# Moving elementwise work to the scalar engine and sums over partitions back to the matrix engine in a four-layer graph network

## The chip, the cores and the metric

The kernel runs on one core of a Trainium2 chip. A core has five engines that each work through their own instruction stream in the order in which it was written: PE (TensorE, matmuls), DVE (VectorE, elementwise work and reductions), ACT (ScalarE, activations and copies), POOL (GpSimd, slower elementwise work[...]) and SP (here it only issues DMAs). They meet through semaphores. Matmul results land in PSUM, of which this kernel has eight buffers of 128 x 512 float32; everything else lives in SBUF.

The metric is the device time of one execution in microseconds, given as the median over runs. All arithmetic is float32.

## The reference, cut to what matters

64 independent graphs of 256 nodes with 256 features go through four layers, each of the form `x = layernorm(x + layer(x, adj))`. What the change touches, in the reference's own terms with the rest cut:

```python
# layer 0: leaky ReLU (slope 0.01) on three projections, sigmoid attention, normalized by degree
X = heads(lrelu(x @ W_lin + b_lin)); q = heads(lrelu(x @ W_q)); k = heads(lrelu(x @ W_k))
adj_h = adj[:, None] * sigmoid(q @ k.T * scale)          # 4 heads
deg = sum(adj_h, axis=-1); dis = where(deg > 0, deg ** -0.5, 0)
Y = (dis[..., :, None] * adj_h * dis[..., None, :]) @ X  # then a layernorm with gain and bias
# layer 1: masked softmax attention with 8 heads
scores = where(adj > 0, q @ k.T / sqrt(32), NEG)
# ...
# layer 2: neighbour sum, then an MLP of width 1024 with an RMS norm
h = agg @ W1 + b1
h = silu(h * rsqrt(mean(h * h, axis=-1) + 1e-6) * rms_weight); out = h @ W2 + b2
# layer 3: additive attention
e = s1[:, :, None] + s2[:, None, :]; e = where(e > 0, e, 0.2 * e); e = where(adj > 0, e, NEG)
h_prime = softmax(e) @ Wh
hn = (h_prime - mean) / sqrt(var + 1e-5) * gamma + beta; out = gelu(hn)
```

## The kernel before: the parts that matter

The kernel describes each graph's work as a list of operations, each with an engine, a cost that its author assigned, and the values it reads and writes. A list scheduler in the kernel then takes the operations of all 64 graphs together, picks at each step the one that can start first, and emits them in that order. So the order on each engine is fixed when the program is built, and several graphs at different layers are in flight at once. `"p"` values are PSUM buffers (eight), `"s"` values are SBUF buffers, `"h"` values are scratch in device memory.

```python
SLOTS = {"s": 42, "d": 10, "b": 3, "c": 72, "p": 8, "h": 8}

def transposed(src):                    # four 128x128 transposes on PE, into PSUM
    ps = Value("p", "ps", 2)
    transpose(lambda: two(ps), lambda: two(src), ps, src)
    return ps

def far_transposed(src, name):          # a transpose by DVE in 32x32 blocks, a DMA out and four DMAs back
    eb, far, dst = Value("s", "eb"), Value("h", "far"), Value("s", name, 4)
    op("DVE", 600, lambda: dve.transpose(...), [eb], [src])
    op("SP", 420, lambda: nc.sync.dma_start(far.t[:, :512], eb.t), [far], [eb], after=3000)
    for q in range(4):
        op("SP", 420, lambda q=q: nc.sync.dma_start(dst.t[...], far.t[...]), [(dst, q)], [far], after=4200)
    return dst

def normed(src, name):                  # layernorm: statistics on DVE, power -0.5 on POOL, apply on DVE
    mv, m = stats(src)
    dst = Value("s", name, 2)
    for n in range(NB):
        op("DVE", 328, lambda n=n: dve.tensor_scalar(two(dst)[:, n, :], two(src)[:, n, :],
           m()[:, n, 0:1], m()[:, n, 2:3], op0=OP.subtract, op1=OP.mult), [(dst, n)], [(src, n), mv])
    return dst

# ---- layer 0
for w, name in ((lambda: c.w0_q, "qT0"), (lambda: c.w0_k, "kT0")):
    ps = feature_major(w, xT)
    y = Value("s", name)
    op("ACT", 478, lambda ps=ps, y=y: act.activation(y.t, ps.t, AF.Copy, scale=0.01), [y], [ps])
    op("DVE", 608, lambda ps=ps, y=y: dve.tensor_tensor(y.t, ps.t, y.t, OP.max), [y], [ps, y])
# ... v likewise: bias on DVE, then max(0.01 v, v) on DVE
added = [Value("s", "added") for _ in range(H0 // 2)]
for i in range(2):                      # POOL adds the two halves of the key index
    op("POOL", 1220, lambda i=i, A2=A2: pool.tensor_tensor(two(added[i]), A2(0), A2(1), OP.add), ...)
def fn(ps=ps):                          # PE sums over partitions with a matrix of ones
    for h in range(H0):
        pe.matmul(ps.t[h * 32:(h + 1) * 32, :N], c.ones, two(added[h // 2])[:, h % 2], start=True, stop=True)
op("PE", PE_MM, fn, [ps], added, mode="columns")
# ...
yb = far_transposed(ps, "yT")
# ... two DVE multiplications by dis, each 128x256, then layernorm

# ---- between layers 0 and 1
op("DVE", 343, lambda: dve.tensor_scalar(adj.t, adj.t, 0.0, NEG, op0=OP.is_le, op1=OP.mult), [adj], [adj])

# ---- layer 2
for j in range(0, HB, 2):               # HB = 8
    # ... two blocks of W1 into ps, then
    op("DVE", 608, lambda ps=ps, j=j: dve.tensor_tensor(
        Hb(j, 2), two(ps), c.b2_1[:, j:j + 2, None].to_broadcast([P, 2, N]), OP.add), both, [ps])
    sq = Value("s", "sq")
    op("ACT", 532, lambda sq=sq, j=j: act.activation(two(sq), Hb(j, 2), AF.Square), [sq], both)
    sqs.append(sq)
    if len(sqs) % 2 == 0:               # POOL adds the squares of this pair and the one before
        op("POOL", 1220, lambda a=sqs[-2], sq=sq: pool.tensor_tensor(sq.t, sq.t, a.t, OP.add), [sq], [sq, sqs[-2]])
# then four matmuls with ones, one column group each

# ---- layer 3
# low3 = 0.2 * s1 on DVE; e = 0.2 * s2 + low3 on ACT; e = max(s2 + s1, e) on DVE
for n in range(NB):                     # 1/sum of the softmax
    op("DVE", 392, lambda n=n, ps=ps: dve.tensor_scalar(two(y3)[:, n, :], two(ps)[:, n, :], r3.t[:, n:n + 1], None,
                                                        op0=OP.mult), [(y3, n)], [(ps, n), r3])
mv, m = stats(y3)
affine(y3, mv, m, lambda: c.g3, lambda n: c.b3)
```

Of the kernel before, what the change touches and what calls it, by code (L numbers as in the profile page):

```python
# [10 lines left out]
AF = mybir.ActivationFunctionType  # L11
OP = mybir.AluOpType
# [151 lines left out]
def graph(plan, nc, c, t, out, b):  # L164
# [32 lines left out]
    def far_transposed(src, name):  # L197


        eb, far, dst = Value("s", "eb"), Value("h", "far"), Value("s", name, 4)  # L200
        op("DVE", 600, lambda: dve.transpose(
            eb.t.rearrange("p (b g i) -> p g b i", b=4, i=32),
            src.t.rearrange("p (n k w) -> p k n w", n=2, k=2)), [eb], [src])
        op("SP", 420, lambda: nc.sync.dma_start(far.t[:, :512], eb.t), [far], [eb], after=3000)
        for q in range(4):
            op("SP", 420, lambda q=q: nc.sync.dma_start(
                dst.t[32 * q:32 * q + 32].rearrange("j (a g) -> j a g", a=4),
                far.t[:, :512].rearrange("(a j) (b g) -> b j a g", a=4, b=4)[q]), [(dst, q)], [far], after=4200)
        return dst

    def spread(v):

        return v.t.rearrange("p (a j i w) -> p j i a w", a=4, j=2, i=2)

# [5 lines left out]
    def feature_major(w, xT, cols=None):  # L220

        ps = Value("p", "ps", 2)
        for o in range(2):
            def fn(o=o):
                for k in range(DB):
                    pe.matmul(two(ps)[:, o, :], w()[:, k, o * P:(o + 1) * P], (cols or two)(xT)[:, k],  # L226
                              start=(k == 0), stop=(k == DB - 1))
            op("PE", 2 * PE_MM, fn, [(ps, o)], [xT])
        return ps

    def token_major(xT, w, r=(), cols=None):

        ps = Value("p", "ps", 2)
        for n in range(NB):
            def fn(n=n):
                for k in range(DB):
                    pe.matmul(two(ps)[:, n, :], cols(xT)[:, k, n] if cols else two(xT)[:, k, n * P:(n + 1) * P], w()[:, k, :],  # L237
                              start=(k == 0), stop=(k == DB - 1))
            op("PE", 2 * PE_MM, fn, [(ps, n)], [xT, *r])
        return ps  # L240
# [4 lines left out]
    def stats(src):  # L245

        mv, st = Value("c", "mv", 2), Value("c", "st", 2)
        m = lambda: mv.t[:, :6].rearrange("p (n k) -> p n k", n=2)
        for n in range(NB):
            op("DVE", 311, lambda n=n: dve.bn_stats(st.t[:, 6 * n:6 * n + 6], two(src)[:, n, :]), [(st, n)], [(src, n)])  # L250
        for n in range(NB):
            op("DVE", 82, lambda n=n: dve.bn_aggr(m()[:, n, 0:2], st.t[:, 6 * n:6 * n + 6]), [(mv, n)], [(st, n)])  # L252

        def fn():
            pool.tensor_scalar(m()[:, :, 2], m()[:, :, 1], 1e-5, None, op0=OP.add)  # L255
            pool.tensor_tensor(m()[:, :, 2], m()[:, :, 2], c.mhalf[:, :NB], OP.pow)  # L256
        op("POOL", 1750, fn, [mv], [mv])
        return mv, m
# [20 lines left out]
    def affine(y, mv, m, g, add, r=()):  # L279

        for n in range(NB):
            op("DVE", 395, lambda n=n: dve.scalar_tensor_tensor(
                two(y)[:, n, :], two(y)[:, n, :], m()[:, n, 0:1], g(), op0=OP.subtract, op1=OP.mult),
                [(y, n)], [(y, n), mv])
# [21 lines left out]
    for w, name in ((lambda: c.w0_q, "qT0"), (lambda: c.w0_k, "kT0")):  # L306
        ps = feature_major(w, xT)
        y = Value("s", name)
        op("ACT", 478, lambda ps=ps, y=y: act.activation(y.t, ps.t, AF.Copy, scale=0.01), [y], [ps])
        op("DVE", 608, lambda ps=ps, y=y: dve.tensor_tensor(y.t, ps.t, y.t, OP.max), [y], [ps, y])  # L310
# [5 lines left out]
    op("DVE", 608, lambda: dve.scalar_tensor_tensor(v.t, v.t, 0.01, v.t, op0=OP.mult, op1=OP.max), [v], [v])  # L316
# [20 lines left out]
    added = [Value("s", "added") for _ in range(H0 // 2)]  # L337
    for i in range(2):
        A2 = lambda n, i=i: att.t.rearrange("p (h n c) -> p h n c", h=H0, n=NB)[:, 2 * i:2 * i + 2, n]
        op("POOL", 1220, lambda i=i, A2=A2: pool.tensor_tensor(two(added[i]), A2(0), A2(1), OP.add),  # L340
           [added[i]], [(att, 2 * i), (att, 2 * i + 1)])

    def fn(ps=ps):
        for h in range(H0):
            pe.matmul(ps.t[h * 32:(h + 1) * 32, :N], c.ones, two(added[h // 2])[:, h % 2], start=True, stop=True)
    op("PE", PE_MM, fn, [ps], added, mode="columns")
# [26 lines left out]
    yb = far_transposed(ps, "yT")  # L373
    y = Value("s", "y", 2)
    for i in range(2):
        by = lambda ap, i=i: ap.rearrange("p g (i k w) -> p g i k w", i=2, k=2)[:, :, i]
        op("DVE", 345, lambda y=y, i=i, by=by: dve.tensor_tensor(
            by(y.t.rearrange("p (g d) -> p g d", g=4)), yb.t.rearrange("p (i k g w) -> p i g k w", i=2, k=2, g=4)[:, i],
            dis.t[:, :8].rearrange("p (g i) -> p i g", i=2)[:, i, :, None, None].to_broadcast([P, 4, 2, 32]), OP.mult),
            [y], [yb, dis])  # L380
# [5 lines left out]
    op("DVE", 343, lambda: dve.tensor_scalar(adj.t, adj.t, 0.0, NEG, op0=OP.is_le, op1=OP.mult), [adj], [adj])  # L386
# [81 lines left out]
    for j in range(0, HB, 2):  # L468
        ps = Value("p", "ps", 2)
        for i in range(2):  # L470
# [6 lines left out]
        op("DVE", 608, lambda ps=ps, j=j: dve.tensor_tensor(  # L477
            Hb(j, 2), two(ps), c.b2_1[:, j:j + 2, None].to_broadcast([P, 2, N]), OP.add), both, [ps])
# [4 lines left out]
        if len(sqs) % 2 == 0:  # L483
            op("POOL", 1220, lambda a=sqs[-2], sq=sq: pool.tensor_tensor(sq.t, sq.t, a.t, OP.add), [sq], [sq, sqs[-2]])  # L484

    def fn(sqs=sqs):
        for i in range(4):
            pe.matmul(sums.t[i * 32:(i + 1) * 32, :N], c.ones, two(sqs[i // 2 * 2 + 1])[:, i % 2, :],
                      start=True, stop=True)
    op("PE", PE_MM, fn, [sums], [sqs[1], sqs[3]], mode="columns")  # L490
# [51 lines left out]
    low3 = Value("c", "low3")  # L542
    op("DVE", 50, lambda: dve.tensor_scalar(low3.t[:, :NB], V3()[:, :, D], 0.2, None, op0=OP.mult), [low3], [v3])
# [6 lines left out]

    e = Value("s", "e3", 2)
    for n in range(NB):
        op("ACT", 360, lambda n=n: act.activation(two(e)[:, n, :], ps2.t[:, :N], AF.Identity,
                                                  bias=low3.t[:, n:n + 1], scale=0.2), [(e, n)], [ps2, low3])
        op("DVE", 395, lambda n=n: dve.scalar_tensor_tensor(
            two(e)[:, n, :], ps2.t[:, :N], s1(n), two(e)[:, n, :], op0=OP.add, op1=OP.max),
            [(e, n)], [(e, n), ps2, v3])
# [6 lines left out]
    for n in range(NB):  # L564
        op("DVE", 392, lambda n=n, ps=ps: dve.tensor_scalar(two(y3)[:, n, :], two(ps)[:, n, :], r3.t[:, n:n + 1], None,
                                                            op0=OP.mult), [(y3, n)], [(ps, n), r3])
    mv, m = stats(y3)
    affine(y3, mv, m, lambda: c.g3, lambda n: c.b3)
# [140 lines left out]
```

## Time and profile before

| | |
|---|---|
| time, median of 3 runs | 3073.91 us (3069.96 to 3080.2) |
| span of the profiled run | 3068.2 us, mean granted clock of PE 0.980 |
| busy: PE, DVE, ACT, POOL | 2887.1, 2714.1, 1783.9, 1241.2 us |
| DMA | 412.31 MB, mean 134 GB/s |

A row of the group view reads: line of the kernel, engine, operation, output <- inputs, shape, count | busy time and mean nanoseconds of one | idle time of the engine just before these instructions, and what ended it. One float32 matmul in the source stands as two MATMUL instructions in the trace, each with its weight load (row PEld). Matmuls are pipelined: the trace gives each a length of about 380 ns, but they start 216 ns apart in a dense stretch, so the distance of the starts counts and not the length. PSUM buffers carry the name `ps` nearly everywhere.

### The profile page before, as it was taken

To read this page: it belongs to the slowest core of one execution; us is meant where nothing else is said; L and a number is where in the kernel's file an instruction comes from. 1 tells how busy PE (TensorE), PEld (TensorE's weight loads), DVE (VectorE), ACT (ScalarE), POOL (GpSimd) and SP (SyncE) were. 2 spreads that over 40 slices of the span, in tenths; PEclk is the share of its full clock that TensorE was granted. 3 is DMA by queue.
4 is the path that set the end of the run, shared out by engine and by line. 5 is a ranking of instruction groups with operands and counts; after the bars stand their busy time and mean duration, and the time that the engine had idled before them with its cause. 6 is when DMAs were issued, how large, how long until landed. Compare 5 with 4: busy or idle time off the path is not lost.

```text
span 3068.2 us, 55984 instructions
## 1 busy us (share of the span) xinstructions
PE 2887.1 (94%) x17860; PEld 2230.5 (73%) x17860; DVE 2714.1 (88%) x7693; ACT 1783.9 (58%) x4226; POOL 1241.2 (40%) x1478
## 2 busy tenths in 40 slices
PE   4899999999999999999999999998999999998986
PEld 3677777777778777777777777776777777776764
DVE  3879999999989989989788999988998999899874
ACT  1545656666556566655556656655566556555553
POOL 3234444444434434344334443443444443443322
PEclk8999999999999999999999999999999999999997
DMA  5444455443554445535353454354454455353440
GB/s 165 134 137 147 131 146 162 131 135 109 148 151 149 151 130 146 148 111 155 94 162 104 152 155 145 113 143 124 135 155 138 124 168 152 100 147 118 124 124 11
DMA packets 351766, 412.31 MB, mean 134 GB/s; under 512 B 42992, under 2 KB 310128, under 8 KB 351472
## 3 DMA queue, kind: packets, MB, share of 16 engines
q1 hardware_dynamic: 344064, 403.34, 44.8%
q10 hardware_dynamic: 7408, 5.39, 0.6%
q8 instruction: 144, 2.36, 0.3%
q14 instruction: 150, 1.23, 0.1%
HBM read 240.27 MB, written 168.30 MB: 133 GB/s over the span
## 4 chain that ended last, share of the span: by engine, by line
PE 56%; DVE 28%; DMA 7%; issue 2%; SPq 2%; ACT 2%; POOL 2%; DVEq 0%; POOLq 0%; ACTq 0%
PE ps L473 10%; PE ps L522 9%; PE ps L226 9%; PE ps L237 8%; PE ps L405 3%; PE ps L537 3%; DVE eb L417 3%; DVE st L250 3%; DVE x L264 2%; DVE e L294 2%; PE ps L370 2%; DVE att L334 2%; PE ps L327 2%; PE av L430 2%; DVE hT L509 2%
## 5 line engine op out<-in xcount | busy, mean ns | idle before, releaser
L299 ACT ACTIVATE e<-e,low 128x256 f32<-128x256 f32 x1152 | 573.7, 501 | 83.4 <-DVE low L294 82.2
L522 PE MATMUL ps<-L_gnn_W,hT 128*128 128x256 f32 x2048 | 481.7, 387 | 18.7 <-ACT hT L513 18.7
L473 PE MATMUL ps<-aggT,L_gnn_W 128*128 128x256 f32 x2048 | 480.1, 382 | 2.6 <-DVE hT L477 1.1
L522 PEld LDWEIGHTS ps<-L_gnn_W,hT 128*128 128x128 f32 x2048 | 383.9, 191 | 100.5 <-ACT hT L513 23.4
L473 PEld LDWEIGHTS ps<-aggT,L_gnn_W 128*128 128x128 f32 x2048 | 378.8, 190 | 67.9 <-issue 10.0
L294 DVE CUSTOM_DVE_ANT_0 e<-ps,adj 128x256 f32<-128x256 f32 x1024 | 363.7, 417 | 23.4 <-PE ps L405 22.8
L484 POOL TENSOR_TENSOR sq<-sq 128x512 f32<-128x512 f32 x128 | 168.5, 1317 | 483.6 <-ACT sq L480 477.2
L255 POOL TENSOR_SCALAR mv<-mv 128x2 f32<-128x2 f32 x384 | 123.7, 322 | 580.9 <-DVE mv L252 526.1
L417 DVE STREAM_TRANSPOSE eb<-e 128x1024 f32<-128x1024 f32 x256 | 310.5, 1222 | 8.2 <-ACT e L299 8.2
L256 POOL TENSOR_TENSOR mv<-mv,mhalf 128x2 f32<-128x2 f32 x384 | 297.4, 774 | 32.0
L250 DVE BATCH_NORM_STATS2 st<-y 128x6 f32<-128x256 f32 x768 | 288.6, 410 | 1.7
L271 POOL TENSOR_TENSOR xb<-x,b 128x512 f32<-128x512 f32 x128 | 175.5, 1372 | 213.2 <-DMA x<-in_x 140.3
L340 POOL TENSOR_TENSOR added<-att 128x512 f32<-128x512 f32 x128 | 179.5, 1406 | 158.8 <-DVE att L334 122.2
L299 ACT ACTIVATION_READ_ACCUMULATOR e<-e,low 128x1 f32 x1152 | 219.1, 190 | 0.0
L509 DVE SCALAR_TENSOR_TENSOR hT<-hT,r,pr 128x256 f32<-128x256 f32 x512 | 205.3, 473 | 7.4 <-PE pr L506 7.3
L334 DVE TENSOR_TENSOR att<-att,adjT 128x512 f32<-128x512 f32 x256 | 197.4, 798 | 13.1 <-DMA adjT<-in_adjT 7.7
L264 DVE TENSOR_SCALAR x<-y,mv 128x256 f32<-128x256 f32 x384 | 183.8, 506 | 16.5 <-POOL mv L256 16.5
L480 ACT ACTIVATE sq<-hT 128x512 f32<-128x512 f32 x256 | 157.8, 622 | 69.2 <-DVE hT L477 66.6
L217 ACT COPY xT<-ps 128x512 f32<-128x512 f32 x128 | 74.6, 582 | 196.2 <-PE ps L189 189.7
L477 DVE TENSOR_TENSOR hT<-ps,b 128x512 f32<-128x512 f32 x256 | 169.3, 681 | 14.5 <-PE ps L473 13.8
L332 ACT ACTIVATE att<-ps 128x512 f32<-128x512 f32 x256 | 135.6, 598 | 75.5 <-PE ps L327 75.0
L358 POOL TENSOR_TENSOR dp<-dp,mhalf 128x8 f32<-128x8 f32 x64 | 109.2, 1707 | 144.8 <-DVE dp L357 139.6
(109 smaller groups left out, 6136.3 us busy)
## 6 DMA issues: line engine op xcount, KB each, us to landing
far<-eb SPq DMA_DIRECT2D x256, 512.0 KB, 3.0
eT<-far SPq DMA_DIRECT2D x1024, 128.0 KB, 3.8
x0T<-in_xT SPq DMA_DIRECT2D x64, 256.0 KB, 4.1
adjT<-in_adjT SPq DMA_DIRECT2D x64, 256.0 KB, 4.1
x<-in_x SPq DMA_DIRECT2D x64, 256.0 KB, 4.4
adj<-in_adj SPq DMA_DIRECT2D x64, 256.0 KB, 3.9
far<-eb SPq DMA_DIRECT2D x64, 256.0 KB, 2.2
yT<-far SPq DMA_DIRECT2D x256, 64.0 KB, 2.2
```

Of the source, the lines that this page charges most:

```text
L226: pe.matmul(two(ps)[:, o, :], w()[:, k, o * P:(o + 1) * P], (cols or two)(xT)[:, k], start=(k == 0), stop=(k == DB - 1))
L237: pe.matmul(two(ps)[:, n, :], cols(xT)[:, k, n] if cols else two(xT)[:, k, n * P:(n + 1) * P], w()[:, k, :], start=(k == 0), stop=(k == DB ...
L250: op("DVE", 311, lambda n=n: dve.bn_stats(st.t[:, 6 * n:6 * n + 6], two(src)[:, n, :]), [(st, n)], [(src, n)])
L256: pool.tensor_tensor(m()[:, :, 2], m()[:, :, 2], c.mhalf[:, :NB], OP.pow)
L264: op("DVE", 328, lambda n=n: dve.tensor_scalar(two(dst)[:, n, :], two(src)[:, n, :], m()[:, n, 0:1], m()[:, n, 2:3], op0=OP.subtract, op1= ...
L294: op("DVE", 345, lambda n=n: dve.tensor_tensor_reduce(out=E(n), in0=two(logits)[:, n, :], in1=two(negmask)[:, n, :], scale=-scale, scalar= ...
L299: op("ACT", 491, lambda n=n: act.activation(E(n), E(n), AF.Exp, bias=low.t[:, n:n + 1], scale=-1.0, accum_out=r.t[:, col(n):col(n) + 1]), ...
L334: op("DVE", 608, lambda h=h: dve.tensor_tensor(A(h), A(h), two(adjT), OP.mult), [(att, h)], [(att, h), adjT])
L417: op("DVE", 1130, lambda e=e, eb=eb: dve.transpose(eb.t.rearrange("p (b g i) -> p g b i", b=4, i=32), e.t.rearrange("p (g b i) -> p g b i" ...
L473: pe.matmul(two(ps)[:, i, :], c.w2_1[:, k, (j + i) * P:(j + i + 1) * P], two(aggT)[:, k, :], start=(k == 0), stop=(k == DB - 1))
L509: op("DVE", 391, lambda j=j: dve.scalar_tensor_tensor(Hb(j)[:, 0], Hb(j)[:, 0], c.r2[:, j:j + 1], pr.t[:, :N], op0=OP.mult, op1=OP.mult), ...
L522: pe.matmul(two(ps)[:, n, :], Hb(j)[:, 0, n * P:(n + 1) * P], c.w2_2[:, j, :], start=(j == 0), stop=(j == HB - 1))
```

## The change

The change takes work off DVE and puts it on ACT, POOL and PE. (1) The leaky ReLUs of layer 0 and of layer 3 become one parametric-ReLU activation on ACT each. (2) The softmax's 1/sum in layer 3 is no longer multiplied into the rows; it enters the statistics of the norm that follows. (3) Layer 2's bias is added on ACT. (4) Layer 1's mask is made on POOL. In return three things that had relieved PE are gone: (5) the two additions on POOL ahead of layer 0's degree sums, (6) the two ahead of layer 2's sums of squares, and (7) layer 0's transpose by way of DVE and device memory, in whose place PE transposes.

```diff
-        op("ACT", 478, lambda ps=ps, y=y: act.activation(y.t, ps.t, AF.Copy, scale=0.01), [y], [ps])
-        op("DVE", 608, lambda ps=ps, y=y: dve.tensor_tensor(y.t, ps.t, y.t, OP.max), [y], [ps, y])
+        op("ACT", 478, lambda ps=ps, y=y: act.activation(y.t, ps.t, AF.Prelu, alpha=0.01), [y], [ps])
...
-    op("DVE", 608, lambda: dve.scalar_tensor_tensor(v.t, v.t, 0.01, v.t, op0=OP.mult, op1=OP.max), [v], [v])
+    op("ACT", 478, lambda: act.activation(v.t, v.t, AF.Prelu, alpha=0.01), [v], [v])
...
-        op("POOL", 1220, lambda i=i, A2=A2: pool.tensor_tensor(two(added[i]), A2(0), A2(1), OP.add),
-           [added[i]], [(att, 2 * i), (att, 2 * i + 1)])
...
-        for h in range(H0):
-            pe.matmul(ps.t[h * 32:(h + 1) * 32, :N], c.ones, two(added[h // 2])[:, h % 2], start=True, stop=True)
-    op("PE", PE_MM, fn, [ps], added, mode="columns")
+        for m in range(NB):
+            for h in range(H0):
+                pe.matmul(ps.t[h * 32:(h + 1) * 32, :N], c.ones, A(h)[:, m, :], start=(m == 0), stop=(m == NB - 1))
+    op("PE", 2 * PE_MM, fn, [ps], [att], mode="columns")
...
-    yb = far_transposed(ps, "yT")
+    ps = transposed(copy(ps, "yT"))
     y = Value("s", "y", 2)
-    for i in range(2):   # ... two multiplications by dis, from yb
+    op("DVE", 608, lambda ps=ps, y=y: dve.tensor_tensor(by_head(y.t), by_head(ps.t), dis_b(), OP.mult), [y], [ps, dis])
...
-    op("DVE", 343, lambda: dve.tensor_scalar(adj.t, adj.t, 0.0, NEG, op0=OP.is_le, op1=OP.mult), [adj], [adj])
+    op("POOL", 1100, lambda: pool.tensor_scalar(adj.t, adj.t, 0.0, NEG, op0=OP.is_le, op1=OP.mult), [adj], [adj])
...
-        op("DVE", 608, lambda ps=ps, j=j: dve.tensor_tensor(
-            Hb(j, 2), two(ps), c.b2_1[:, j:j + 2, None].to_broadcast([P, 2, N]), OP.add), both, [ps])
+        for i in range(2):
+            op("ACT", 357, lambda ps=ps, i=i, j=j: act.activation(
+                Hb(j + i)[:, 0], two(ps)[:, i, :], AF.Identity, bias=c.b2_1[:, j + i:j + i + 1]), [(hT, j + i)], [(ps, i)])
...
-        if len(sqs) % 2 == 0:
-            op("POOL", 1220, lambda a=sqs[-2], sq=sq: pool.tensor_tensor(sq.t, sq.t, a.t, OP.add), [sq], [sq, sqs[-2]])
...
+        if len(sqs) == 2:               # twice per graph: four matmuls with ones, summed up in one PSUM buffer
+            def fn(sqs=sqs, j=j):
+                for i in range(4):
+                    pe.matmul(sums.t[i * 32:(i + 1) * 32, :N], c.ones, two(sqs[i // 2])[:, i % 2, :],
+                              start=(j == 2), stop=(j == HB - 2))
...
-    op("DVE", 50, lambda: dve.tensor_scalar(low3.t[:, :NB], V3()[:, :, D], 0.2, None, op0=OP.mult), [low3], [v3])
...
-        op("ACT", 360, lambda n=n: act.activation(two(e)[:, n, :], ps2.t[:, :N], AF.Identity,
-                                                  bias=low3.t[:, n:n + 1], scale=0.2), [(e, n)], [ps2, low3])
-        op("DVE", 395, lambda n=n: dve.scalar_tensor_tensor(
-            two(e)[:, n, :], ps2.t[:, :N], s1(n), two(e)[:, n, :], op0=OP.add, op1=OP.max),
-            [(e, n)], [(e, n), ps2, v3])
+        op("ACT", 360, lambda n=n: act.activation(two(e)[:, n, :], ps2.t[:, :N], AF.Prelu, bias=s1(n), alpha=0.2),
+           [(e, n)], [ps2, v3])
...
-        op("DVE", 392, ...)             # y3 = ps * r3, twice
-    mv, m = stats(y3)
-    affine(y3, mv, m, lambda: c.g3, lambda n: c.b3)
+    mv, m = stats(ps, r3)               # three small DVE products put r3 into variance and scale
+    affine(y3, mv, m, lambda: c.g3, lambda n: c.b3, src=ps)
```

## The prediction

> **What bounds the kernel now.** I read the busy line of the page first, then the same engines cut into head, middle and tail, then the waits of PE, then the rows of each line that the change touches, and last a piece of PE's timeline.
>
> ```profile
> PE 2887.1 (94%) x17860; PEld 2230.5 (73%) x17860; DVE 2714.1 (88%) x7693; ACT 1783.9 (58%) x4226; POOL 1241.2 (40%) x1478
> ...
> core 0: us, PE busy (x) PEld busy (x) DVE busy (x) ACT busy (x) POOL busy (x), PEclk, DMA share, GB/s
> 0.00:200.00 200.00, 148.72 (x885) 110.01 (x886) 128.51 (x332) 75.38 (x179) 62.67 (x75) 0.91 0.50 145
> 200.00:2800.00 2600.00, 2522.71 (x15770) 1956.37 (x15769) 2392.11 (x6792) 1577.42 (x3752) 1099.18 (x1300) 0.99 0.47 139
> 2800.00:3068.00 268.00, 215.64 (x1208) 164.13 (x1207) 193.47 (x571) 131.07 (x296) 79.35 (x105) 0.90 0.28 85
> ```
>
> In the middle 2600 us PE is busy for 2522.7, that is 97%, and idle for only 77 us. DVE is at 92% there. Of PE's 181 idle us (3068.2 - 2887.1), 51 lie in the first 200 us (weights still arriving) and 52 in the last 268 (the last graphs have no others to hide behind). So the kernel is bound by PE, with DVE close behind as the engine that PE sometimes waits for:
>
> ```profile
> PE ps L189 <- DVE x L264: 34.9, 34, 3.7
> PE ps L327 <- DVE kT L310: 19.5, 1, 19.5
> PE ps L522 <- ACT hT L513: 18.7, 7, 5.7
> PE ps L657 <- DMA b_v<-in_L_gnn_bv: 18.2, 1, 18.2
> PE ps L189 <- DVE mv L252: 8.3, 4, 5.6
> ```
>
> Columns: who waits for whom, total us, how often, longest. The two single waits of 18 to 20 us belong to the start. What repeats is PE waiting for a normalized `x` (L264) before it can transpose it. The whole list is short: PE has enough other graphs to work on.
>
> ```profile
> 1004.65 6.21 PE L473 MATMUL ps<-aggT,L_gnn_W 128*128 128x256 f32 x28
> 1010.70 0.60 PE L189 MATMUL ps<-ident,e 128*128 128x128 f32 x4
> 1011.14 1.89 PE L226 MATMUL ps<-x0T,L_gnn_W_k 128*128 128x256 f32 x8
> ...
> 1015.55 0.64 PE L488 MATMUL sums<-sq,ones 128*32 128x256 f32 x8
> 1016.01 0.61 PE L345 MATMUL ps<-added,ones 128*32 128x256 f32 x8
> 1016.55 1.13 PE L237 MATMUL ps<-L_gnn_Wo,yT 128*128 128x256 f32 x4
> ```
>
> These are prices: start to next start, not the printed lengths. A full matmul instruction takes 6.05 / 28 = 216 ns, four transposes 0.44 us, eight instructions of a sum over partitions (four column groups at once, two passes) 0.46 us, or 0.54 when the array goes back to full matmuls afterwards.
>
> **What the Trainium skill says.** "Perfetto Trace Analysis", section Tensor Engine Instruction, says that the profiler estimates a matmul's end; hence my prices from starts. The trace agrees: rows give 380 to 400 ns for instructions that start 216 ns apart. "TensorEngine Tiling (Array Packing)", Key Properties, says that changing the tiling mode drains the array. The 0.08 us between the two sums above fit that, though they are one sample. "SBUF — State Buffer", section SBUF: two separate sides, says that DVE and GpSimd share a port pair held exclusively for a whole instruction. The trace shows something of the kind: L264, a DVE operation from SBUF, has a median of 404 ns but a mean of 506 and a maximum of 1385, and a POOL addition on 128x512 takes 1317 to 1406. "ScalarE: Activation LUTs", section Table sets, lists relu, copy and identity as members of every table set; it does not name parametric ReLU. The order of the changed program answers that: it holds the same 258 table loads as before (67 + 62 + 64 + 64 + 1), so I charge none.
>
> **The change part by part.**
>
> ```profile
> L477 DVE TENSOR_TENSOR hT<-ps,b 128x512 f32<-128x512 f32 x256 | 169.3, 681 | 14.5 <-PE ps L473 13.8
> L484 POOL TENSOR_TENSOR sq<-sq 128x512 f32<-128x512 f32 x128 | 168.5, 1317 | 483.6 <-ACT sq L480 477.2 <-PE ps L473 6.3
> L340 POOL TENSOR_TENSOR added<-att 128x512 f32<-128x512 f32 x128 | 179.5, 1406 | 158.8 <-DVE att L334 122.2 <-DVE mv L252 7.8 <-DVE low L543 7.6
> L377 DVE TENSOR_TENSOR y<-yT,dis 128x256 f32<-128x256 f32 x128 | 69.8, 550 | 2.1 <-DMA yT<-far 2.1
> L565 DVE TENSOR_SCALAR y<-ps,r 128x256 f32<-128x256 f32 x128 | 59.7, 473 | 39.0 <-PE ps L237 38.1 <-POOL sq L484 0.6
> L553 ACT ACTIVATE e<-ps,low 128x256 f32<-128x256 f32 x128 | 53.4, 469 | 26.8 <-PE ps L548 16.4 <-DVE low L543 6.1 <-DVE low L294 1.1
> ```
>
> DVE loses, in us of busy time: the leaky ReLU products 42.7 + 42.4 (L310) and 50.5 (L316); the block transpose 44.8 (L201); the two multiplications 69.8 (L377); the mask 33.4 (L386); layer 2's bias 169.3 (L477); layer 3's 16.2 (L543), 55.7 (L555) and 59.7 (L565). That is 584. It gains one multiplication from PSUM (64 x 0.67, as L276 takes 674 ns, = 43) and three tiny products (64 x 3 x 0.14, as L359 takes 142 ns, = 27). Net -514 us: 2714 becomes about 2200. Fewer POOL additions should also shorten L264: if half of its excess of about 0.1 us over the median goes, that is another 25 us over 512 instructions.
>
> ACT gains the bias, 512 x 0.469 (L553 has the same shape, PSUM source and bias pointer) = 240; the ReLU of `v`, 64 x 0.62 (L480) = 40; the copy ahead of the new transpose, 64 x 0.58 = 37. 1784 becomes about 2100, 68% of the span. The two ReLUs from PSUM replace copies of the same shape (594 ns) and cost nothing more.
>
> POOL loses 168.5 + 179.5 and gains the mask. For that I take 1.1 us, a guess below the two-input additions, so 70 us. 1241 becomes about 960. The DMA queue loses 64 stores of 256 KB and 256 loads of 64 KB, 33.6 of 412 MB.
>
> PE, the bound, gains per graph: eight more instructions for the degrees (0.46), eight more for the squares (0.46), four transposes (0.44). Times 64: 29.4 + 29.4 + 28.2 = 87 us. In the order of the changed program the array's mode changes 1279 times, exactly as often as before, because the second sum of squares and the new transposes mostly land beside others of their kind. So no extra for switching. If nothing else changed, the span would be 3068 + 87 = 3155.
>
> Against that stands what the lighter DVE gives back. Only PE's idle time can come back, and not all of it. Of the 77 us in the middle I expect half, 38: L264 and its statistics stand for most of what repeats, and DVE falls from 92% to about 70% there. From pauses too short to show as idle, since a 380 ns printed length covers a start that is late by up to 160 ns, I guess 10. From head and tail I take 9: in the last graph's layer 3 the chain loses L543 (0.25), the second pass of L555 after L553 (about 0.9) and L565 ahead of the norm (about 0.9), in layer 2 a POOL addition (1.3), and three or so graphs drain one behind the other. Sum 57. Net +30 us on a median of 3073.9: 3104 us, 1.0% slower.
>
> **The rivals.** (a) DVE is the real bound and PE only looks full, because printed lengths overlap. Then 514 us less DVE would buy much more than 57, and the time would fall to about 3000. For it: 92% on DVE in the middle, and 28% of the chain of waits on DVE. Against it: 28 dense matmuls really start 216 ns apart, and PE's waits for DVE sum to some tens of us. (b) Nothing comes back: the plan was already tight, what idles is the start, the end and the DMAs, and the whole 87 us show: 3155 to 3160. For it: only 77 us are idle in the middle. Against it: the L264 waits, which a DVE with slack should cut. (c) ACT becomes the new source of waits. It now frees the PSUM buffers of layer 2's first matmul, in order behind exponentials with 1152 x (0.50 + 0.19) us and table loads of 1.28 us; a PSUM buffer of layer 3 is also kept through the whole norm, and `sums` is held from the first half on. PE would then stall for PSUM: 3140 to 3170. For it: eight PSUM buffers, all in demand. Against it: ACT stays below 70%, and layer 0's ReLU buffers come free one operation earlier.
>
> **Range and chances.** Full recovery of the middle with 20 more from the ends gives about 3074 + 87 - 107 = 3054; none gives 3161. I put four fifths of the weight between 3068 and 3140, since both extremes need every small effect to point one way. Faster by over 2% (below 3012) needs rival (a): 0.03. Slower by over 2% (above 3135) needs (b) or (c): 0.13. Within 2%: 0.84.
>
> **What would show it.** Right, if the changed profile has DVE at about 2150 to 2200 us, ACT near 2100, POOL near 960, PE's busy time up by 60 to 90 us, the middle's PE share at 98% or more, and L189 waiting for the norm clearly less than 34.9 us. The prices are wrong if the two sums take more than about 1.0 us per graph each. The mechanism is wrong if PE's busy share in the middle stays at 97% or falls while DVE sinks below 75%: then the waits did not come from DVE's load. New waits of PE for ACT at layer 2's first matmul would show rival (c).

## The result and the profile after

The changed kernel takes 3025.62 us (median of 4 runs, 3018.84 to 3027.26) against 3077.05 us (3069.96 to 3080.22) for the kernel before in the same series: a ratio of 0.9832, 95% interval 0.9807 to 0.9857. It is 1.7% faster. The prediction said 3104 us, with 3068 to 3140 as its range, so its sign was wrong.

The busy line of the changed kernel's page, and the same engines cut into head, middle and tail as before (the columns are those of the three windows in the prediction):

```profile
PE 2925.9 (97%) x19140; PEld 2281.5 (76%) x19140; DVE 2236.8 (74%) x6925; ACT 2019.2 (67%) x4866; POOL 1002.0 (33%) x1286
```

```profile
core 0: us, PE busy (x) PEld busy (x) DVE busy (x) ACT busy (x) POOL busy (x), PEclk, DMA share, GB/s
0.00:200.00 200.00, 170.34 (x1133) 130.30 (x1134) 121.11 (x358) 108.21 (x263) 67.33 (x76) 0.97 0.51 153
200.00:2750.00 2550.00, 2518.51 (x16604) 1968.83 (x16604) 1938.76 (x6012) 1749.39 (x4232) 873.78 (x1115) 1.00 0.44 127
2750.00:3017.00 267.00, 237.06 (x1409) 182.33 (x1403) 176.94 (x558) 161.58 (x374) 60.86 (x95) 0.94 0.30 91
```

PE is now busy for 98.8% of the middle, DVE for 76% of it. PE's idle time went from 51.3 to 29.7 us in the head, from 77.3 to 31.5 in the middle and from 52.4 to 29.9 in the tail: 90 us less.

PE does 87 us more work in a span that is 51 us shorter. So about 139 us of PE's waiting went away, where the prediction had 57. Only 90 of them show as idle time. The busy row grew by 38.8 us instead of 87. The other 48 are pauses that the printed matmul lengths had covered.

PE's waits in the changed kernel (who waits for whom, total us, how often, longest):

```profile
PE ps L189 <- DVE x L256: 23.2, 20, 3.4
PE ps L631 <- DMA b_v<-in_L_gnn_bv: 18.4, 1, 18.4
PE ps L319 <- ACT kT L302: 10.2, 1, 10.2
PE ps L219 <- ACT eT L199: 3.7, 9, 0.7
```

The wait for the normalized `x` fell from 34.9 to 23.2 us. The single wait at the start is now one for ACT's leaky ReLU instead of DVE's, and 9 us shorter (10.2 after 19.5). PE's wait for layer 2's activations at the second matmul of that layer, 18.7 us before, has dropped out of the top: the full list has it at 0.3.

A piece of PE's timeline shows the work that was added (start us, length, engine, line; the second sum, L470, is one of the two halves of layer 2's squares):

```profile
1021.24 1.05 PE L333 MATMUL ps<-att,ones 128*32 128x256 f32 x16
1022.22 1.95 PE L358 MATMUL ps<-att,v 128*64 128x256 f32 x16
1028.77 0.60 PE L189 MATMUL ps<-ident,yT 128*128 128x128 f32 x4
1029.21 1.89 PE L208 MATMUL ps<-xT,L_gnn_Wk 128*128 128x256 f32 x8
1042.21 0.64 PE L470 MATMUL sums<-sq,ones 128*32 128x256 f32 x8
1042.78 1.13 PE L456 MATMUL ps<-aggT,L_gnn_W 128*128 128x256 f32 x4
```

Sixteen instructions for the degrees take 0.98 us from start to next start, the transposes of `yT` 0.44, one half of the squares 0.57. Over the whole trace, start to start and on the mean, the additions per graph are 382 ns for the degrees, 529 for the squares, 444 for the transposes: 86.7 us for 64 graphs, against 87 predicted.

Last, the rows of the operations that moved or got faster (busy us, mean ns, then DVE's, ACT's or POOL's idle time before them and its releaser):

```profile
L369 POOL TENSOR_SCALAR adj<-adj 128x512 f32<-128x512 f32 x64 | 127.5, 1991 | 52.7 <-DMA adj<-in_adj 34.5 <-PE ps L443 4.1 <-DMA far<-eb 4.1
...
L256 DVE TENSOR_SCALAR x<-y,mv 128x256 f32<-128x256 f32 x384 | 163.2, 457 | 24.4 <-POOL mv L246 24.0
...
L302 ACT ACTIVATE qT<-ps 128x512 f32<-128x512 f32 x64 | 38.7, 604 | 28.3 <-PE ps L208 27.7
...
L461 ACT ACTIVATE hT<-ps,b 128x256 f32<-128x256 f32 x512 | 234.2, 471 | 157.9 <-PE ps L456 157.9
```

The parametric ReLU costs 604 ns where the copy it replaces took 594, and the bias 471 ns where 469 was assumed. The mask takes 1.99 us on POOL where 1.1 was guessed. The norm's apply step, the instruction that subtracts the mean and scales, has a mean of 457 ns, down from 506.

### The profile page after: what moved, and what is told of

The parts are those of the page before. It is cut to its first block, busy times and chain, and to the rows that moved or that the text cites. A ratio compares the mean times of both kernels' runs of the same rounds, so it can differ in the third digit from the quotient of the medians.

```text
span 3017.0 us, 57099 instructions
## 1 busy us (share of the span) xinstructions
PE 2925.9 (97%) x19140; PEld 2281.5 (76%) x19140; DVE 2236.8 (74%) x6925; ACT 2019.2 (67%) x4866; POOL 1002.0 (33%) x1286
## 4 chain that ended last, share of the span: by engine, by line
PE 79%; DVE 10%; ACT 6%; DMA 3%; issue 1%; POOL 1%; SPq 0%; ACTq 0%; DVEq 0%; POOLq 0%
PE ps L208 14%; PE ps L219 13%; PE ps L456 12%; PE ps L505 12%; PE ps L388 4%; PE ps L189 3%; PE ps L443 3%; PE ps L358 3%; PE ps L319 3%; PE av L413 3%; PE ps L520 3%; ACT e L292 3%; PE sums L470 2%; DVE st L233 2%; PE ps L333 2%
## 5 line engine op out<-in xcount | busy, mean ns | idle before, releaser
L505 PE MATMUL ps<-L_gnn_W,hT 128*128 128x256 f32 x2048 | 469.0, 383 | 0.3 <-ACT hT L496 0.3
L461 ACT ACTIVATE hT<-ps,b 128x256 f32<-128x256 f32 x512 | 234.2, 471 | 157.9 <-PE ps L456 157.9
L246 POOL TENSOR_TENSOR mv<-mv,mhalf 128x2 f32<-128x2 f32 x384 | 287.6, 749 | 32.0
L233 DVE BATCH_NORM_STATS2 st<-y 128x6 f32<-128x256 f32 x640 | 242.8, 415 | 4.3
L292 ACT ACTIVATION_READ_ACCUMULATOR e<-e,low 128x1 f32 x1152 | 229.8, 199 | 0.0
L492 DVE SCALAR_TENSOR_TENSOR hT<-hT,r,pr 128x256 f32<-128x256 f32 x512 | 205.4, 473 | 20.8 <-PE pr L489 20.5
L326 DVE TENSOR_TENSOR att<-att,adjT 128x512 f32<-128x512 f32 x256 | 170.5, 697 | 21.3 <-ACT att L324 21.3
L256 DVE TENSOR_SCALAR x<-y,mv 128x256 f32<-128x256 f32 x384 | 163.2, 457 | 24.4 <-POOL mv L246 24.0
L484 POOL TENSOR_TENSOR rs<-rs,mhalf 128x2 f32<-128x2 f32 x64 | 46.1, 720 | 377.4 <-DVE rs L483 358.7
L496 ACT ACTIVATE hT<-hT 128x1024 f32<-128x1024 f32 x128 | 131.6, 1053 | 40.4 <-DVE hT L492 31.8
L219 PE MATMUL ps<-v,eT 128*128 128x256 f32 x512 | 141.4, 408 | 8.3 <-ACT eT L199 3.7
```

What stands on the lines that cost most here:

```text
L219: pe.matmul(two(ps)[:, n, :], two(xT)[:, k, n * P:(n + 1) * P], w()[:, k, :], start=(k == 0), stop=(k == DB - 1))
L292: op("ACT", 491, lambda n=n: act.activation(E(n), E(n), AF.Exp, bias=low.t[:, n:n + 1], scale=-1.0, accum_out=r.t[:, col(n):col(n) + 1]), ...
L326: op("DVE", 608, lambda h=h: dve.tensor_tensor(A(h), A(h), two(adjT), OP.mult), [(att, h)], [(att, h), adjT])
L461: op("ACT", 357, lambda ps=ps, i=i, j=j: act.activation(Hb(j + i)[:, 0], two(ps)[:, i, :], AF.Identity, bias=c.b2_1[:, j + i:j + i + 1]), ...
L492: op("DVE", 391, lambda j=j: dve.scalar_tensor_tensor(Hb(j)[:, 0], Hb(j)[:, 0], c.r2[:, j:j + 1], pr.t[:, :N], op0=OP.mult, op1=OP.mult), ...
L505: pe.matmul(two(ps)[:, n, :], Hb(j)[:, 0, n * P:(n + 1) * P], c.w2_2[:, j, :], start=(j == 0), stop=(j == HB - 1))
```

## The experiments

Three theories stand against each other. The **load theory**, the prediction's own: what came back is what a lighter DVE gives back, only more of it. The **collision theory**: what came back is mostly the collisions of POOL's two-input additions on 128x512 with DVE operations whose data lie in SBUF, so it belongs to parts 5 and 6 and not to DVE's load. The **order theory**: the order of the schedule is one of many, and 1.7% is a lucky one. The expectations are quoted as they were written ahead of each batch of runs; where they give a theory a letter or another name, the words beside it say which is meant.

The seven parts fall into three groups: **D** (parts 1 to 4, work off DVE), **S** (parts 5 and 6, sums on PE, no additions on POOL; +58.8 us of PE) and **Y** (part 7, layer 0's transpose on PE; +28.2 us of PE). Each kernel below was compared with the kernel before in three rounds on the same chip; "ratio" is to that kernel. Two measures were worked out from all instructions of a trace. *Excess* is the sum of DVE instruction time above the median of the same line and operation, counted where it is over 200 ns. *PE's pauses* is the time from PE's first to last matmul start less the dense price of all of them; changes of the array's shape, which cost about 97 ns each in these traces, are still in it.

### Which group brings it: all combinations

The kernels undo or apply hunks of the printed diff as they stand. `e1` is D alone, `e2` is S and Y without D, `e4` is part 3 alone, `e6` is the changed kernel without Y, `e9` the changed kernel without S, `e10` is S alone, `e11` is Y alone. The cores of the two that matter most, as edits of the changed kernel (`e9`) and of the kernel before (`e11`):

```diff
# e9: POOL's additions are back, the sums read them (layer 2 likewise)
+        op("POOL", 1220, lambda i=i, A2=A2: pool.tensor_tensor(two(added[i]), A2(0), A2(1), OP.add),
+           [added[i]], [(att, 2 * i), (att, 2 * i + 1)])
...
-    op("PE", 2 * PE_MM, fn, [ps], [att], mode="columns")
+    op("PE", PE_MM, fn, [ps], added, mode="columns")
# e11: only the transpose of layer 0 goes to PE
-    yb = far_transposed(ps, "yT")
+    ps = transposed(copy(ps, "yT"))
... (and the multiplication by dis)
```

> Parts 1 to 4 alone (work taken off DVE); the POOL additions and layer 0's transpose through device memory stay. Theory A (DVE's load was the source of PE's lost time, visible and hidden, and the added matmuls cost their full 87 us): the changed kernel's 3026 less about 80 us, 2945 us (2930 to 2965). Rival B (the relief comes from parts 5 to 7: POOL and DMAs off the path, fewer round trips): hardly better than the kernel before, 3040 to 3075 us.

> Parts 5 to 7 alone (additions on POOL gone, layer 0 transposed on PE); DVE's work stays, but for about 70 us. Theory A: 87 us of new PE work at nearly full price, 3135 to 3160 us. Rival B: these parts bring the relief, 3020 to 3060 us.

> Part 3 alone: layer 2's bias moves from DVE (169 us) to ACT (about 240 us). Theory A: a third of DVE's relief, so a third or somewhat more of the 133 us that came back, 3015 to 3040 us. Rival C (ACT frees these PSUM buffers late and PE waits for it): 3075 us or more.

> The changed kernel with part 7 undone: layer 0's transpose goes through DVE and device memory again, 28 us less on PE. Theory L: the 28 us less show in part, 2995 to 3020 us. Theory T: the round trip costs more than PE saves, 3045 us or more.

> The changed kernel with parts 5 and 6 undone: POOL adds again ahead of both sums over partitions, and PE has 59 us less to do. Collisions alone (the spare additions cost 24 us): 2985 to 3000 us. Theory D (the addition stands between the values and the sum, so the sum, the power after it and all that follows wait for POOL's turn; more than PE's 59 us are lost): 3035 to 3065 us.

> Parts 5 and 6 alone, on the kernel before: 59 us more on PE. Collisions alone: 3075 + 59 - 24, 3100 to 3115 us. Theory D: the 59 us come back in full or more, 3045 to 3075 us.

> Part 7 alone, on the kernel before: 28 us more on PE, no round trip through device memory. From the changed kernel, where undoing it won 11 us of the 28: 3080 to 3095 us. If the round trip mattered more while DVE was loaded: 3075 us or less.

"Returned" is the price of the group's PE work plus what the time fell, so it is the waiting that went away. The last columns are PE's waits summed over the whole list by who ended them.

| kernel | groups | ratio, 95% | PE price | returned, us | PE waits for DVE / POOL, us |
|---|---|---|---|---|---|
| before | | 1 | 0 | 0 | 100 / 3 |
| e1 | D | 0.9914 [0.9896, 0.9933] | 0 | 26 | 80 / 5 |
| e10 | S | 0.9961 [0.9951, 0.9971] | 59 | 71 | 67 / 0 |
| e11 | Y | 1.0176 [1.0158, 1.0195] | 28 | -26 | 73 / 46 |
| e2 | S, Y | 0.9974 [0.9959, 0.9989] | 87 | 95 | 83 / 1 |
| e6 | D, S | 0.9797 [0.9781, 0.9812] | 59 | 121 | 24 / 7 |
| e9 | D, Y | 0.9565 [0.9544, 0.9587] | 28 | 162 | 25 / 7 |
| after | D, S, Y | 0.9832 [0.9807, 0.9857] | 87 | 139 | 31 / 1 |
| e4 | part 3 only | 0.9954 [0.9939, 0.9969] | 0 | 14 | 91 / 10 |

Four of these seven expectations missed. `e2` (3075.25 us) and `e4` (3068.51) fell between the ranges of their theories, `e9` (2945.91) below both of its ranges and `e11` (3132.38) above both. `e1` (3055.84) is far from the 2945 of the load theory, in the range by which D hardly helps; `e6` (3012.87) is in the range of the collisions, `e10` (3065.91) in that by which POOL's additions hold up the sums.

Three things follow. First, the groups don't add up in these orders. D and Y change the time by -0.86% and +1.76% alone and by -4.35% together. Second, S pays for itself on the kernel before (59 us of PE work, and the time still falls by 0.4%), but on top of D and Y it costs 82 us, more than its own price: `e9`, without S, is faster than the changed kernel by 0.9832 - 0.9565 = 2.7%. Third, part 7 on top of D and S costs 0.35%, and on top of D alone it brings 3.5%. Some of both is changes of the array's shape: the traces have 805 in `e1`, 713 in `e9` and 827 in the changed kernel, which at 97 ns makes 9 us of what Y brings on D and 11 us of what S costs there. The best version is therefore neither kernel but D with Y. The collision theory in its plain form, that the gain sits in S, falls with this.

How Y alone loses can be read in part in its trace. PE's waits in `e11`, then a piece of its timeline (start us, length, engine, line; in brackets the idle time before it and its releaser):

```profile
PE ps L356 <- POOL added L351: 44.5, 24, 2.1
PE ps L189 <- DVE x L274: 21.0, 36, 3.4
```

```profile
1626.73 2.10 POOL L281 TENSOR_TENSOR xb<-x,b 128x512 f32<-128x512 f32 x1
...
1627.63 2.63 DVE L274 TENSOR_SCALAR o<-y,mv 128x256 f32<-128x256 f32 x2
...
1628.80 1.31 POOL L281 TENSOR_TENSOR xb<-x,c 128x512 f32<-128x512 f32 x1
...
1631.54 1.27 POOL L351 TENSOR_TENSOR added<-att 128x512 f32<-128x512 f32 x1 [1.43 <-DVE att L345]
...
1632.13 1.23 DVE L345 TENSOR_TENSOR att<-att,adjT 128x512 f32<-128x512 f32 x1
...
1633.37 0.65 DVE L345 TENSOR_TENSOR att<-att,adjT 128x512 f32<-128x512 f32 x1
...
1634.19 0.81 POOL L264 TENSOR_TENSOR mv<-mv,mhalf 128x2 f32<-128x2 f32 x1
...
1634.88 1.26 POOL L351 TENSOR_TENSOR added<-att 128x512 f32<-128x512 f32 x1
...
1636.19 0.84 PE L356 MATMUL ps<-added,ones 128*32 128x256 f32 x4 [2.01 <-POOL added L351]
```

Two apply steps of 0.4 us take 2.63 us together beside two additions on POOL, and a product that takes 0.65 us elsewhere takes 1.23 beside a third. POOL's second degree addition doesn't start when its product is ready (1633.37 + 0.65 = 1634.02) but at 1634.88: in POOL's fixed order a norm's power (L264) stands ahead of it, and PE stands for 2 us. In all 24 cases of this wait the product had been ready for 0.85 us. So the wait comes from POOL's order as well as from collisions.

The kernel before doesn't have this wait among its top five. It is 44.5 us. `e11` is 54 us slower, of which 28 are PE's new work, so all waiting rose by 26 only: other waits fell (those for DVE from 100 to 73). With D in place the same additions are there and PE's waits for POOL are 7 us. Why D removes this wait was not taken apart. `e11` was run in one order only, and the wait comes back in it at the same place again and again; whether Y alone loses in another order, and how much of the interaction of D and Y would be left then, is not shown.

### Is it DVE's load?

`e3` puts most of the load back on the changed kernel: 18 more statistics instructions per graph on DVE, which nothing reads, at the places where the removed work stood. If the load theory holds, most of the return is lost again.

```diff
+    def spare(src, n, part=None):
+        o = Value("c", "spare")
+        def fn():
+            for i in range(n):
+                dve.bn_stats(o.t[:, 6 * (i % 2):6 * (i % 2) + 6], src.t[:, 256 * (i % 2):256 * (i % 2) + 256])
+        if n:
+            op("DVE", 311 * n, fn, [o], [src])
...
+    spare(v, 2)
... (and after qT, kT, y, the mask, the squares, e and y3)
```

> The changed kernel with 18 spare statistics operations per graph on DVE (18 x 0.415 x 64 = 478 us, what DVE lost), spread over the places where work left DVE, and with no reader. Theory A1 (the load on DVE's queue is what counts): back to the level of parts 5 to 7 alone, 3110 to 3150 us. Theory A2 (what counts is that steps went out of each graph's chain, whatever DVE does besides): 3025 to 3050 us.

Ratio 0.9848 [0.9832, 0.9864], 3035.34 us, in the range of the theory that steps left each graph's chain (A2). The busy line and the first wait of `e3`:

```profile
PE 2933.3 (97%) x19140; PEld 2277.5 (75%) x19140; DVE 2579.8 (85%) x8077; ACT 2025.6 (67%) x4866; POOL 1003.0 (33%) x1286
```

```profile
PE ps L189 <- DVE x L265: 17.2, 13, 4.3
```

DVE's busy time is up by 343 us, so 72% of the 477 us that it had lost are back, and it is about as loaded as in `e2` (2616 us), which has the same work on PE. Yet `e3` differs from the changed kernel by 0.16%, within the intervals, and PE's wait for `x` is no longer than there. Of the 1.42% by which D improves on `e2`, 1.26% is still there with the load back. So the load theory falls: what D brings is not that DVE is less busy. The limit of this run is that nothing waits for the spare instructions. It tests occupation, not the length of the chains that D also shortens.

### What POOL's additions cost

`e5` puts four additions per graph on POOL back into the changed kernel, written to spare buffers, while PE keeps its longer sums. `e8` puts four other POOL instructions in the same places: a power on 128x8, which occupies POOL for longer but reads little. `e7` goes the other way and moves the remaining large POOL work, the residual additions and the mask, to DVE. `e12` does that with the residual additions of the kernel before, where DVE is the fullest. `e18` does it on `e9`.

```diff
# e5
+        op("POOL", 1220, lambda spare=spare, A2=A2: pool.tensor_tensor(two(spare), A2(0), A2(1), OP.add),
+           [spare], [(att, 2 * i), (att, 2 * i + 1)])
...
+            op("POOL", 1220, lambda a=sqs[-2], sq=sq, spare=spare: pool.tensor_tensor(spare.t, sq.t, a.t, OP.add), [spare], [sq, sqs[-2]])
# e8
+        op("POOL", 1610, lambda spare=spare, i=i: pool.tensor_tensor(spare.t[:, :8], att.t[:, 1024 * i:1024 * i + 8], c.mhalf, OP.pow),
+           [spare], [(att, 2 * i), (att, 2 * i + 1)])
... (and the same on the squares)
# e7, e18, and without the mask e12
-        op("POOL", 1220, lambda: pool.tensor_tensor(two(xb), two(x), row_b(r()), OP.add), [xb], [x])
+        op("DVE", 608, lambda: dve.tensor_tensor(two(xb), two(x), row_b(r()), OP.add), [xb], [x])
...
-    op("POOL", 1100, lambda: pool.tensor_scalar(adj.t, adj.t, 0.0, NEG, op0=OP.is_le, op1=OP.mult), [adj], [adj])
+    op("DVE", 343, lambda: dve.tensor_scalar(adj.t, adj.t, 0.0, NEG, op0=OP.is_le, op1=OP.mult), [adj], [adj])
```

> The changed kernel with the four POOL additions of 128x512 per graph put back as spare work: same inputs, result without a reader, PE's sums as in the changed kernel. Theory L (a long POOL operation and a DVE operation on SBUF hold each other up; these delays, which the plan does not know, are what PE lost): DVE's long outliers back from 62 us towards 150 us or more, and the time 3080 to 3130 us. Theory T (the round trip of layer 0's transpose through device memory was the cost): 3025 to 3040 us.

> The changed kernel with four spare powers of 128x8 per graph on POOL (about 1.65 us each, so as much of POOL's time as the four additions, but hardly any SBUF data), at the places of the additions, without a reader. Theory L: no collisions, 3025 to 3045 us. Theory Q (POOL's queue: work ahead of the norms' powers delays them): like the additions, 3080 us or more.

> The changed kernel with the three residual additions of each graph (128x512, 192 in all) and the mask moved from POOL to DVE, so that POOL keeps only small operations; DVE gets about 150 us more work. Theory L: DVE's outliers vanish and PE gets back 40 to 60 us, 2960 to 2990 us. A rival by which slack on DVE counts, or spread over engines: 3030 us or more.

> The kernel before with its three residual additions per graph moved from POOL to DVE (115 us more DVE, which stands at 88%). If collisions cost more than load: outliers fall from 175 to about 100 us and the time to 3045 to 3065 us. If DVE at over 90% sets the pace: 3090 us or more.

> e9 with the residual additions and the mask on DVE as in e7; POOL keeps the additions ahead of the sums. Collisions fall by half, DVE stays below 85%: 10 to 35 us less than e9, 2910 to 2936 us. If DVE's load counts more: 2946 us or more.

| kernel | ratio, 95% | DVE busy, us | excess, us | PE's pauses, us |
|---|---|---|---|---|
| before | 1 | 2714 | 175 | 397 |
| e12, residual additions to DVE | 0.9877 [0.986, 0.9893] | 2756 | 110 | 371 |
| after | 0.9832 [0.9807, 0.9857] | 2237 | 62 | 264 |
| e5, additions on POOL added | 0.9909 [0.9894, 0.9924] | 2319 | 146 | 297 |
| e8, powers on POOL added | 0.981 [0.9794, 0.9827] | 2226 | 63 | 261 |
| e7, large POOL work to DVE | 0.9796 [0.9781, 0.9811] | 2293 | 1 | 257 |
| e9 | 0.9565 [0.9544, 0.9587] | 2315 | 131 | 250 |
| e18, e9 with large POOL work to DVE | 0.9529 [0.9509, 0.9548] | 2371 | 86 | 240 |

Rows of `e5` and of `e8` (the apply step and the added instructions on the scores) and of `e7` (the apply step):

```profile
L256 DVE TENSOR_SCALAR x<-y,mv 128x256 f32<-128x256 f32 x384 | 190.7, 529 | 14.0 <-POOL mv L246 13.7
...
L332 POOL TENSOR_TENSOR spare<-att 128x512 f32<-128x512 f32 x128 | 172.1, 1348 | 51.7 <-DVE att L326 44.8 <-issue 3.2 <-DMA rb<-far 3.0
```

```profile
L331 POOL TENSOR_TENSOR spare<-att,mhalf 128x8 f32<-128x8 f32 x128 | 222.7, 1742 | 20.5 <-DVE att L326 19.7 <-DMA eT<-far 0.8
...
L256 DVE TENSOR_SCALAR x<-y,mv 128x256 f32<-128x256 f32 x384 | 165.1, 465 | 40.1 <-POOL mv L246 39.7
```

```profile
L256 DVE TENSOR_SCALAR x<-y,mv 128x256 f32<-128x256 f32 x384 | 142.1, 401 | 16.7 <-POOL mv L246 14.8
```

The apply step takes 401 ns on the mean when POOL does no large operation, 457 with the residual additions, 529 with four more additions, and still 465 with four powers that each hold POOL for 1742 ns. So what lengthens the DVE step is not that POOL is occupied, it is the large operation. In the kernel before, all 229 instructions with an excess overlap one of POOL's additions on 128x512 or 128x128; ten of them overlap one of its powers too, none a power alone. Two inputs aren't needed: in the changed kernel 25 of 92 such instructions overlap the mask and no addition. The additions agree with the shared port pair that the prediction cited from the Trainium skill ("SBUF — State Buffer", section SBUF: two separate sides): the 84 apply steps of the kernel before that overlap a 128x512 addition and nothing else have a median of 1.35 us, as long as the addition itself. The powers don't agree with a pair that is held for the whole of any POOL instruction: in `e8`, 203 apply steps beside a power have a median of 405 ns.

Its effect on the time is real and limited. Putting the additions back costs 0.77% (24 us), a ratio above those of all three orders of the changed kernel (below), so about that much of the 139 can be put down to them. `e5` also fills spare SBUF buffers of full size, which `e8` doesn't; that rival was not separated. Both `e5` (3048.33 us) and `e7` (3014.08) fell between their two expected ranges: collisions cost less than expected. `e8`, `e12` and `e18` came within 8 us of the ranges of the collision theory. And `e9` has twice the excess of the changed kernel and is 82 us faster. Moving work to DVE helps in all three kernels, by 1.23%, 0.36% and 0.36%. The two small steps are no larger than what another order of the same work does (below); the first is larger. The most telling is `e12`: DVE goes to 91% busy and the time falls by 38 us. PE's wait for the normalized `x` there is down from 34.9:

```profile
PE 2883.5 (95%) x17860; PEld 2226.5 (73%) x17860; DVE 2756.3 (91%) x7885; ACT 1786.5 (59%) x4226; POOL 991.9 (33%) x1286
```

```profile
PE ps L189 <- DVE x L264: 14.1, 11, 3.4
```

The collision theory is thus right on the mechanism, and too large a claim as the whole cause.

### Is it the order?

Every edit reshuffles the fixed order. Two constants of the scheduler were changed slightly, one at a time, to get other orders of the same work: on the kernel before (`e13`, `e14`), on the changed kernel (`e15`, `e16`) and the first one on `e9` (`e17`).

```diff
# e13, e15, e17
-AFTER = {"PE": 230, "DVE": 150, "ACT": 190, "POOL": 180, "SP": 3000}
+AFTER = {"PE": 230, "DVE": 150, "ACT": 195, "POOL": 180, "SP": 3000}
# e14, e16
-CHANGE = {"full": 0, "rows": 100, "columns": 140, "transpose": 60}
+CHANGE = {"full": 0, "rows": 105, "columns": 140, "transpose": 60}
```

> The kernel before with one number in the scheduler's table changed (how long after an ACT operation its result is seen: 195 instead of 190), so the same instructions in another order. Theory M (the work decides): within 15 us of the kernel before, 3062 to 3092 us. Theory S (the order decides as much as the work): 25 us or more away on either side.

> The kernel before with another number changed (105 instead of 100 for a change of PE into row mode): again only the order. Theory M: 3062 to 3092 us. Theory S: 25 us or more away.

> The changed kernel with the first of these two numbers changed. Theory M: within 15 us of the changed kernel, 3010 to 3040 us. Theory S: 25 us or more away.

> The changed kernel with the second number changed. Theory M: 3010 to 3040 us. Theory S: 25 us or more away. If the two families of orders don't overlap, the gain of the change is in the work and not in its order.

> e9 with the scheduler's number changed as in e13 and e15: the same work in another order. If e9's gain is in the work: within 15 us of it, 2930 to 2962 us. If its order was lucky: 2970 us or more, nearer to what e1 and the changed kernel let one expect.

| work | order as given | constant 1 | constant 2 |
|---|---|---|---|
| before | 1 | 1.0054 [1.0035, 1.0072] | 1.0056 [1.0036, 1.0075] |
| after | 0.9832 [0.9807, 0.9857] | 0.9813 [0.9799, 0.9828] | 0.985 [0.9833, 0.9866] |
| e9 | 0.9565 [0.9544, 0.9587] | 0.9504 [0.9482, 0.9527] | not run |

In the five orders that were tried, an order is worth up to about 0.6%. The two of the kernel before are 17 us slower than it, just outside the 15 us that were expected. The three families stay apart by more than that, so the order theory falls for the change as a whole and for `e9`. It also says how small differences are to be read: single steps below 0.6%, such as the 0.35% of part 7 on top of D and S, `e7` against the changed kernel, or the falls of `e2`, `e4` and `e10`, can't be told from an order by their time alone. That 59 us of PE's work come back in `e10` is well above it. `e1`, `e2`, `e6`, `e10` and `e11` were run in one order each. `e17` is the fastest version that was run, at 2928.89 us; its busy line:

```profile
PE 2837.7 (97%) x18116; PEld 2256.7 (77%) x18116; DVE 2306.4 (79%) x6925; ACT 2004.5 (68%) x4866; POOL 1313.5 (45%) x1542
```

PE is as full as in the changed kernel, with 1024 matmuls less. POOL holds all its additions.

## Why the prediction was wrong, point by point

**What bounds the kernel.** Right: PE. It went from 97% to 98.8% of the middle.

**Price of the new PE work, 87 us.** Right: 86.7. No extra for mode switches was right too, though not by its count. The 1279 changes of both orders include those between full matmuls and transposes, 522 in the kernel before, at which the starts show no extra time (median 0 ns). Changes of the array's shape do cost time, about 97 ns, and there are 812 before and 827 after.

**Where the removed work goes.** DVE 2237 us (predicted about 2200), ACT 2019 (2100), POOL 1002 (960, with a mask at 1.99 instead of 1.1 us). The 258 table loads are still 258. All near enough. The expected gain on the apply step, 25 us of busy time, came at 49 ns x 384 = 19 us on its larger row.

**"Against that stands what the lighter DVE gives back."** This is the step that failed, in its size and in its mechanism. Its three terms (the middle's idle time, the short pauses, head and tail), 38 + 10 + 9 = 57 us, measured 46 + 48 + 44 = 138.

- The middle (38) was nearly right at 46.
- Head and tail (9) measured 22 + 22. Nearly half of the head was in the profile that the prediction quoted: PE waited 19.5 us for `kT` behind DVE's queue at the start, and part 1 takes that operation off DVE. The wait is 10.2 us with part 1 and was passed over as "belonging to the start". In `e1`, D alone, it is 9.3; in `e2`, without D, 20.5.
- The short pauses (10, called a guess) measured 48. They can't be read from a busy row, since a printed length of 380 ns covers them. From the starts they can: before, the time from PE's first to last matmul start held 397 us more than the dense prices. The 812 changes of shape at about 97 ns are 79 of it; the other 318 are pauses, where the busy row showed 181 us of idle time. The prediction had the prices and didn't take this sum. Some 23 of the 48 may be PE's clock (an estimate, in the last section).

And the mechanism, that a lighter DVE gives this time back, was wrong. `e3` gives DVE 343 us of load back and keeps nearly all of the return. `e12` makes DVE busier than it is in the kernel before and gains 1.2%. `e2`, without D, already returns 95 of the 139, and `e10`, with S alone, 71. About 24 us of the return are collisions with POOL's additions, by `e5`. The remaining 115 are not split further by a run, and their cause stays open. The length of DVE's steps inside chains that PE waits for is the candidate, since D's gain on `e2` survives the load of `e3`, but no run lengthens these chains alone. Nor is the interaction settled by which D and Y bring 162 us back together, while D alone brings 26 and Y alone loses.

**Rival (a), DVE is the real bound, about 3000 us.** Its number was a third as far from the result as the prediction's (26 against 78 us), by luck: its reason is refuted by `e3` and `e12`. **Rival (b), nothing comes back, 3155 to 3160**, and **rival (c), ACT becomes the new wait**: wrong. PE's idle time ahead of layer 2's first matmul is 1.6 us (2.6 before), and its wait for the activations ahead of the second fell from 18.7 to 0.3 us.

**The tests it set itself.** PE's share of the middle above 98% and L189's wait clearly below 34.9 came true, and would have been read as proof of the mechanism. One failed: PE's busy time rose by 38.8 us and not by 60 to 90, the sign that pauses under the printed lengths had closed. None of them can tell a lighter DVE from a less disturbed one. Only the runs that change load and collisions separately do.

**The sum.** 3074 + 87 - 57 = 3104 predicted; with the measured return 3077 + 87 - 139 = 3025.

## What to carry to other kernels

Before charging new work on the bounding engine in full, sum its start-to-start times and subtract the dense price of what it runs: that, less the changes of the array's shape, is the most that can come back, and not the idle time: here 318 us and not 181. An engine's busy share doesn't say what it costs others; test it by putting spare load on it, and look for instructions far above the median of their own line and for what overlaps them. When a change has several parts, run them in combination: here one pair of parts brought 4.4% and the third took 2.7% back.

## What the runs showed of the hardware

- A large operation on POOL lengthens a DVE operation on SBUF. The apply step takes 0.40 us; beside a two-input addition on 128x512 it takes 1.35 in the median and 1.46 at most (kernel before), beside the one-input mask alone up to 0.84 (changed kernel). Beside a power on 128x8, 1.74 us long, it stays at 0.41 (`e8`).
- A mask with two operations on one 128x512 input takes 1.99 us on POOL, more than an addition of two such inputs (1.35).
- A change of the array's shape, between full matmuls and groups of rows or columns, costs about 97 ns in the median (so do changes of the groups' width, counted with them); from full matmuls to groups it is 309 ns from start to start, where 216 is usual. The kernel before has 812 such changes, `e1` 805, `e9` 713. A change between full matmuls and transposes costs nothing: 216 ns from start to start into the transposes, 109 out of them, as within a stretch.
- PE's granted clock falls to half for stretches of 3.4 us or multiples of it (the last one is cut off where the trace ends), and full matmuls then start 427 ns apart instead of 216. The kernel before has 14 of these stretches (122 us), the changed one 6 (47 us), `e11` 24 (125 us). Half of the matmul time within them is an estimate of the loss: 35 us before, 12 after, so some 23 of the 48 us of hidden pauses may be clock and not waiting.
